# A four-layer spectral network and a dilation on one core: loads placed ahead, accumulations moved by one VectorE operation, other first pairs of a layer

## The chip, the cores and the metric

The kernel runs on one core of a Trainium2 chip. The metric is the device time of the program in microseconds (us), as the median of several executions. The profile is a trace of one further execution. PE is TensorE (its matmuls), PEld its weight loads, DVE VectorE, ACT ScalarE, POOL GpSimd and SP SyncE; SP works on no data here, it issues DMAs.

## What is computed

Eight images of 8 channels and 256x256 pixels, all in 32-bit floats. Each is normalized, goes through a Fourier neural operator with four groups of 10 channels, is added to its input, and is normalized and dilated (the maximum over 3x3 pixels):

```python
h = _gconv1x1(h, fc0_w, fc0_b)
for i in range(4):
    h1 = _spectral_conv(h, sp_w1[i], sp_w2[i])   # rfft2, 12x12 low modes mixed by channel, irfft2
    h2 = _gconv1x1(h, w_w[i], w_b[i])
    h = h1 + h2
    if i < 3:
        h = _gswish(h, betas[i])
h = _gswish(_gconv1x1(h, fc1_w, fc1_b), betas[3])
return _gconv1x1(h, fc2_w, fc2_b)
...
x = x + _L0_conv_ref(_gn(x), ...)
x = x + _L1_conv_ref(_gn(x))
```

## The kernel before

Two streams of work are woven into each other. While the layers of image b run, the head of image b-1 (the two 1x1 convolutions fc1 and fc2) runs beside them, and after it the dilation of image b-2 or b-1, called the tail. Image 0 has no head beside it, and the head of image 7 runs alone at the end.

**The head** is a generator of 128 steps. Step n does `first(n)`: four matmuls of 512 columns (L686) into four PSUM banks, a single one and a group of three, which ACT turns into `act` (L687, L688). Each odd step also does `second(n-3)`: eight matmuls (L708) that take two earlier `act` tiles, and an addition of the result to `y` on DVE (L711 for the first of 16, else L713). Below, F36 is `first(36)`, S34 is `second(34)` and y34 its addition.

**A layer** l of an image has four stages. `spectrum_h` turns the rows of the previous layer with four DVE transposes (L353), multiplies them on PE (`p_b`, L362) and scales the result into B with six small DVE operations (L369). `mix` makes twelve DVE operations in turn, a multiplication with spectral weights (L390) and a sum (L393), then F (L405, L406), the small product `p_f` on PE (L415) and from it `fz`, with one DVE multiplication by a mask `own` (L428). `rows_of` makes `p_g` on PE in three groups (G0, G4, G8; L447 in even layers, L452 in odd ones) and copies them to `zt` (L204). `layer` then makes eleven bursts Z0 to Z10 (`p_z`: L523 in layer 0, where the weights are `wcn`, L526 in the others, then L529), which ACT evicts to `h` (L534); in layers 0 to 2 a pair of bursts is turned by DVE (`turn`, L477), transformed by PE (`transform`, L494: D0 to D5) and gathered (`gather`, L508). For layer 0 of the next image, `start` (its spectrum and its mix) runs beside the end of layer 3.

**The order** on PE, DVE and ACT is the order in which the program is written; the generators' `yield`s say how many head steps go in at that place, `"tail"` takes one step of the tail. The order of SP's queue is left to the framework's scheduler. PSUM has two single banks and two groups of three; a new tile takes the one that was freed first in the program's order, so which wait a matmul gets depends on where the reader of an earlier tile stands. A burst, a head step, `p_d` and `p_g` take one bank of each sort; `p_f`, `p_b`, `p_u` and the result of `second` a single one.

**Loads:** `hs` are chunks of layer 3's result, stored to memory and read back for the head; `y` is the part of the input to which the head adds; `read_x` loads the image for layer 0 into `h`; `load_sw` loads the spectral weights for the mix (three parts; the third goes in when the first is used up).

Of the kernel before, what the change touches and what calls it, by code (L numbers as in the profile page):

```python
# [19 lines left out]
HW = 256  # L20
NPIX = HW * HW
G = 4
# [21 lines left out]
def fno_dilate_kernel(ctx: ExitStack, tc: tile.TileContext, a: dict, out: bass.AP):  # L44
    nc = tc.nc
    mm = nc.tensor.matmul
    PE, DVE, ACT = mybir.EngineType.PE, mybir.EngineType.DVE, mybir.EngineType.Activation

# [74 lines left out]
    nc.vector.memset(fz, 0.0)  # L123
    own = const.tile([128, NQ], F32, tag="own", name="own")
    nc.vector.memset(own, 0.0)
    for i in range(NQ):
        nc.vector.memset(own[part(i), i : i + 1], 1.0)

# [218 lines left out]
    def spectrum_h(b, l, out_):  # L347

        rows = turned.rearrange("p t f -> p (t f)")[:, : NBLK * WID * 128]
        view = rows.rearrange("p (g i k) -> p i g k", g=G, k=32)  # L350
        for g in range(G):

            nc.vector.transpose(  # L353
                rows[:, 960 * g : 960 * (g + 1)].rearrange("p (i r) -> p i r", r=32), windows(g))
            yield (1,) if g < G - 1 else (1, 1)
        p = ps_a(f"p_b_{b}_{l}")
        for k in range(2):
            for n in range(2 * NBLK):
                term, blk = n // NBLK, n % NBLK
                for q in range(4):  # L360
                    k0 = 12 * term + 3 * q
                    mm(p[part(q), 120 * k : 120 * k + 120], eh_f[:, spectrum_table(k, term), blk, :],  # L362
                       view[:, WID * blk : WID * (blk + 1), :, k0 : k0 + 3],
                       start=n == 0, stop=n == 2 * NBLK - 1)
        bt = sb.tile([128, 2, 3, G, WID], F32, tag="B", bufs=1, name=f"B_{b}_{l}")
        s = io[:, 4 * l : 4 * l + 4]
        for part_ in range(2):
            for k in range(3):
                nc.vector.tensor_tensor(  # L369
                    bt[:, part_, k].rearrange("p g i -> p i g"),  # L370
                    p[:, 120 * part_ : 120 * part_ + 120].rearrange(
                        "p (i g k) -> p i g k", i=WID, g=G)[:, :, :, k],
                    s.unsqueeze(1).to_broadcast([128, WID, G]), ALU.mult,
                )
        out_["bt"] = bt
# [6 lines left out]
    def mix(b, l, out_):  # L382
# [3 lines left out]
        for n in range(12):  # L386
            k, k2 = n // 4, n // 2 % 2
            pr = turned[:, 2, 1024 * k2 : 1024 * k2 + 800].rearrange("p (g m i) -> p g m i", g=G, i=WID)
            if n % 2 == 0:
                nc.vector.tensor_tensor(  # L390
                    pr, sw[k], bt[:, k2, k].unsqueeze(2).to_broadcast([128, G, 2 * WID, WID]), ALU.mult)
            else:
                nc.vector.tensor_reduce(  # L393
                    s[k2][:, k].rearrange("p g s o -> p (g s o)"),
                    pr.rearrange("p g m i -> p (g m) i"), AX.X, ALU.add,
                )
            if n == 3:
                sw.append(load_sw(l, 2))
            if l > 0:
                if n not in (2, 6, 10):  # L400
                    yield (1,)
            elif n % 2 or n > 7:
                yield (1,)
        f = sb.tile([128, 2, 3, G, WID], F32, tag="F", bufs=1, name=f"F_{b}_{l}")
        nc.vector.tensor_tensor(f[:, 0], s[0][:, :, :, 0, :], s[1][:, :, :, 1, :], ALU.subtract)  # L405
        nc.vector.tensor_tensor(f[:, 1], s[0][:, :, :, 1, :], s[1][:, :, :, 0, :], ALU.add)  # L406
        if l == 0:
            yield (1,)

        p = ps_a(f"p_f_{b}_{l}")  # L410
        sums = p[:, : 6 * WID * G].rearrange("p (o g s k) -> p s o g k", o=WID, g=G, s=2)
        for slot in range(2):
            for n, (table, part_of) in enumerate(((0, slot), (1 + slot, 1 - slot))):
                for q in range(4):
                    mm(sums[part(q), slot], fold[part(q), table, :],  # L415
                       f[part(q), part_of].rearrange("p k g o -> p o g k"), start=n == 0, stop=n == 1)
        nc.vector.tensor_copy(fz[0:32, :, :, 24], cz[:, l])
# [8 lines left out]
        if l < 2:  # L426
            nc.vector.tensor_copy(fz[0:32, :, :, 25], cz[:, 4 if l == 0 else 3])
        nc.vector.tensor_tensor(  # L428
            fz[:, :, :, : 6 * NQ].rearrange("p o g (q k) -> p (o g) q k", q=NQ),
            p[:, : 6 * WID * G].rearrange("p (n k) -> p n k", k=6).unsqueeze(2).to_broadcast([128, WID * G, NQ, 6]),  # L430
            own.unsqueeze(1).unsqueeze(3).to_broadcast([128, WID * G, NQ, 6]), ALU.mult)

    def rows_of(b, l, side):
# [3 lines left out]
        for os_ in (range(0, 4), range(4, 8), range(8, 10)):  # L437
# [16 lines left out]
            for u, o in enumerate(os_):  # L454
# [7 lines left out]
                copy(u, dst, src)  # L462
            yield (1, 1) if os_[0] == 0 or os_[0] == 8 and l < 3 else (1,)
            if l < 3:
                yield "tail"
            elif os_[0] != 4:
                next(side, None)


    def layer(b, l, out_, stored, side):  # L470
# [68 lines left out]

        def read_x(c):  # L540
            for g in range(G):
                nc.sync.dma_start(
                    h[32 * g : 32 * g + 6, c].rearrange("p f w -> p (f w)"), a["xp"][b, c, g])

        if l == 0:
            for c in range(NCH):
                read_x(c)
            wcn = sb.tile([128, 32], F32, tag="wcn", bufs=1, name=f"wcn_{b}")
            nc.vector.tensor_scalar(wcn, wc, out_["mr"][:, 1:2], None, ALU.mult)
        if l == 3:  # L550
            for c in range(NCH):
# [6 lines left out]
                if c in (0, 1, 2, 5, 6, 7):  # L558
                    yield "tail"
                next(side, None)  # L560
            return
        for k in range((NCH + 1) // 2):
# [3 lines left out]
            if k > 1:  # L566
                gather(k - 2)
            if k == 0 or alone[0]:
                turn(c)
# [6 lines left out]
                continue  # L576
            yield (1,)
            turn(c)
            transform(k - 1)
            for _ in range(2 if k > 1 and pair else 1):  # L580
                yield "tail"
# [12 lines left out]
    def start(b, out_):  # L594
        if b < n_img:
            out_["sw"] = [load_sw(0, 0), load_sw(0, 1)]
            yield from spectrum_x(b, out_)
            yield from mix(b, 0, out_)

    def layers(b, stored, d, then):  # L600

# [3 lines left out]
        for l in range(4):  # L605
            if l > 0:
                yield from spectrum_h(b, l, d)
                if l == 3 and b + 1 < n_img:
                    load_x(b + 1)
                yield from mix(b, l, d)  # L610
            yield from rows_of(b, l, then)
            yield from layer(b, l, d, stored, then)
        yield "stored"
        yield from then

# [48 lines left out]


    def head(b, stored, stats):
        hs, acts, box = {}, {}, {}
# [5 lines left out]
        def load_state(k):  # L673

            if k < NQ * NCH:
                j, c = k // NCH, k % NCH
                hs[k] = sb.tile([128, PIX], F32, tag="hs", bufs=4, name=f"hs_{b}_{k}")
                nc.sync.dma_start(hs[k], stored[c][:, PIX * j : PIX * (j + 1)])

        def first(n):  # L680

            k, blk = n // 32 * NCH + n % 32 // NBLK, n % 32 % NBLK
            act = sb.tile([128, G, 512], F32, tag="act", bufs=4, name=f"act_{b}_{n}")
# [7 lines left out]
        def second(n):  # L691

            t, rb = n // 16, n % 16
            if rb == 0:
                if last:
                    y = ya[:, 1 + 2 * t : 3 + 2 * t, 1 : HW + 1]
                else:
                    y = sb.tile([128, 512], F32, tag="yp", name=f"y_{b}_{t}")
                    y = y.rearrange("p (s w) -> p s w", s=2)
                box["y"] = y  # L700
                nc.sync.dma_start(
                    y, a["x"][b].rearrange("c (p t s w) -> (c p) t s w", p=16, t=8, s=2)[:, t])
            y, acc = box["y"], ps_a(f"p_fc2_{b}_{n}")
            sums = acc.rearrange("p (s w) -> p s w", s=2)
            for i in range(2):
                act = acts.pop(n + i)
                for g in range(G):
                    mm(acc[part(g), :], w2[:, g, 15 - rb - i : 47 - rb - i], act[:, g, :],  # L708
                       start=i == 0, stop=i == 1)
            if rb == 0:  # L710
                nc.vector.scalar_tensor_tensor(y, sums, b2, y, ALU.add, ALU.add)  # L711
# [11 lines left out]

        load_state(0)
        load_state(1)
        yield
        for n in range(STEPS):
# [5 lines left out]
            yield  # L733
        second(STEPS - 2)


# [38 lines left out]

    heads, tails, count = [], [], [0]

    def step():
# [4 lines left out]
        if next(gen, b) is b:  # L783
            heads.pop(0)
            tails.append((dilate if b + 1 < n_img else dilate_last)(b, stats_of.pop(b)))
            return step()
        count[0] += 1
        return True
# [6 lines left out]
    with tc.manual_schedule(engines={PE, DVE, ACT}):  # L795
# [3 lines left out]
        for b in range(n_img):  # L799
            stored = [dram.tile([128, NQ * PIX], F32, tag=f"hs{c}", name=f"stored_{b}_{c}") for c in range(NCH)]  # L800
            ahead = {}
            for n in layers(b, stored, d, start(b + 1, ahead)):
                if n == "stored":
                    if b + 1 < n_img:
                        stats_of[b] = sb.tile([128, 8, 6], F32, tag="bn_y", name=f"bn_y{b}")
                    else:
                        stats_of[b] = spare[:, 16384:16480].rearrange("p (n s) -> p n s", s=6)
                    heads.append((b, head(b, stored, stats_of[b])))
                    next(heads[-1][1])
                    alone[0] = False  # L810
                elif n == "tail":
                    tail()
                elif heads:
                    for _ in n:
                        step()
            d = ahead
        while step():
            tail()
        for t in tails:
# [165 lines left out]
```

## Time and profile before

| | |
|---|---|
| Time, median of 3 runs | 3972.9 us (3970.92 to 3978.73) |
| The profiled execution's own time | 3984.03 us |
| Its span | 3982.2 us |
| Granted TensorE clock, mean | 0.960 |
| DMA traffic | read 213.39 MB, written 123.74 MB |
| One head step, first half: 8 records of L686 | 644 ns mean of one, overlapping |
| ACT on one step: L687 and L688 | 601 and 1456 ns |
| One y addition (L713) | 684 ns |
| One multiplication or sum of the mix (L390, L393) | 982 and 984 ns |

The profiled execution was 11 us longer than the median, 0.3%. Each matmul appears as two records[...]. The records of matmuls overlap, so the time of a stage on PE is read from the start of one group to the start of the next. The page names for each engine what ended its idle time. A granted clock below 1.0 means that TensorE ran at half speed for a part of the stretch.

### The profile page before, as it was taken

How to read it: one execution, taken by the hardware profiler on the slowest of the kernel's cores; microseconds unless marked ns; L12 is line 12 of the kernel's file. 1: busy time of each engine (PE TensorE's matmuls, PEld its weight loads, DVE VectorE, ACT ScalarE, POOL GpSimd, SP SyncE). 2: the span in 40 equal slices, each digit the busy share in tenths (PEclk: the TensorE clock that was granted, in tenths of full speed). 3: DMA queues.
4: the chain of work that ended last, by engine and by line, in shares of the span. 5: the costliest groups of instructions: out<-in, count | busy, mean ns of one | idle time of the engine just before them, and what ended most of it. 6: DMA issues, size and time to landing. Idle time of an engine off the chain costs nothing.

```text
span 3982.2 us, 116980 instructions
## 1 busy us (share of the span) xinstructions
PE 3689.1 (93%) x53114; PEld 1427.5 (36%) x53114; DVE 2443.7 (61%) x3675; ACT 2829.6 (71%) x2923; POOL 116.9 (3%) x202
## 2 busy tenths in 40 slices
PE   5669999999999999999999999999999989999997
PEld 2334333333333333333333333333333333333222
DVE  6665665466675666756666566665666556764643
ACT  3336777767777677776777767777777767778886
POOL 1000000000000000000000000000000000000000
PEclk8879999999999999999999999999999989999998
DMA  3014111432125221261213611135112542115321
GB/s 86 15 47 173 51 41 35 164 95 63 59 85 176 62 61 57 80 212 33 63 54 94 198 36 60 56 123 167 56 43 58 163 121 59 56 44 188 110 70 47
DMA packets 114121, 344.94 MB, mean 87 GB/s; under 512 B 16040, under 2 KB 18536, under 8 KB 98200
## 3 DMA queue, kind: packets, MB, share of 16 engines
q1 hardware_dynamic: 95432, 276.32, 22.3%
q0 software_dynamic: 18192, 61.13, 4.7%
q8 instruction: 418, 6.85, 0.7%
q14 instruction: 79, 0.65, 0.1%
HBM read 213.39 MB, written 123.74 MB: 85 GB/s over the span
## 4 chain that ended last, share of the span: by engine, by line
PE 79%; DVE 11%; issue 4%; ACT 4%; DMA 3%; SPq 0%; POOL 0%; DVEq 0%; POOLq 0%; ACTq 0%
PE p_fc L686 22%; PE p_fc L708 21%; PE p_z L529 9%; PE p_d L494 7%; PE p_z L526 6%; PE p_z L523 3%; PE p_u L508 3%; PE p_b L362 2%; DVE turned L477 2%; PE p_g L452 2%; PE p_g L447 2%; PE p_f L415 2%; DVE turned L353 1%; DVE turned L390 1%; DMA t<-in_spw 1%
## 5 line engine op out<-in xcount | busy, mean ns | idle before, releaser
L688 ACT ACTIVATE act<-p_fc 128x1536 f32<-128x1536 f32 x1024 | 1491.2, 1456 | 1.4 <-PE p_fc L686 1.4
L686 PE MATMUL p_fc<-hs,c_w 32*128 32x512 f32 x8192 | 1183.1, 644 | 49.1 <-DVE y L713 22.0
L708 PE MATMUL p_fc<-act,c_w 128*32 128x512 f32 x8192 | 1003.2, 606 | 5.1 <-ACT act L687 4.7
L687 ACT ACTIVATE act<-p_fc 128x512 f32<-128x512 f32 x1024 | 615.1, 601 | 494.2 <-PE p_fc L686 479.4
L477 DVE STREAM_TRANSPOSE turned<-h 128x1024 f32<-128x1024 f32 x528 | 630.3, 1225 | 322.6 <-ACT h L534 322.4
L534 ACT ACTIVATE h<-p_z 128x512 f32<-128x512 f32 (+1 forms) x528 | 511.8, 1021 | 293.1 <-PE p_z L529 293.1
L713 DVE TENSOR_TENSOR y<-p_fc,y 128x512 f32<-128x512 f32 x392 | 268.2, 684 | 569.8 <-PE p_fc L708 569.6
L686 PEld LDWEIGHTS p_fc<-hs,c_w 32*128 32x128 f32 x8192 | 379.5, 187 | 628.4 <-ACT act L687 226.9
L708 PEld LDWEIGHTS p_fc<-act,c_w 128*32 128x32 f32 x8192 | 216.7, 110 | 733.8 <-issue 366.2
L529 PE MATMUL p_z<-c_binv,zt 32*128 32x256 f32 x5632 | 422.1, 415 | 0.0
L529 PEld LDWEIGHTS p_z<-c_binv,zt 32*128 32x128 f32 x5632 | 264.3, 191 | 318.1 <-issue 305.0
L526 PE MATMUL p_z<-h,c_wt 32*32 32x512 f32 x8448 | 353.5, 599 | 6.2 <-ACT act L687 4.1
L494 PE MATMUL p_d<-turned,c_fw 32*32 32x480 f32 (+1 forms) x9216 | 312.2, 541 | 20.9 <-DVE turned L477 20.6
L498 ACT ACTIVATE turned<-p_d 128x1440 f32<-128x1440 f32 x144 | 183.1, 1271 | 101.7 <-PE p_d L494 98.5
L536 ACT ACTIVATE h<-p_z,c_bias 128x512 f32<-128x512 f32 (+1 forms) x176 | 186.6, 1111 | 71.0 <-PE p_z L529 70.8
L204 DVE COPY zt<-p_g 128x264 f32<-128x264 f32 x300 | 161.9, 617 | 95.2 <-PE p_g L447 42.4
L494 PEld LDWEIGHTS p_d<-turned,c_fw 32*32 32x32 f32 x9216 | 129.3, 103 | 201.7 <-issue 66.8
L390 DVE TENSOR_TENSOR turned<-t,B 128x800 f32<-128x800 f32 x192 | 188.5, 982 | 20.5 <-DMA t<-in_spw 20.4
L393 DVE TENSOR_REDUCE S<-turned 128x80 f32<-128x800 f32 x192 | 189.0, 984 | 5.7
L353 DVE STREAM_TRANSPOSE turned<-zt 128x960 f32<-128x960 f32 x96 | 177.4, 1874 | 2.5
L415 PE MATMUL p_f<-F,c_fold 32*32 32x120 f32 x1024 | 62.1, 391 | 102.7 <-DVE F L405 86.9
L526 PEld LDWEIGHTS p_z<-h,c_wt 32*32 32x32 f32 x8448 | 94.1, 103 | 163.5 <-ACT act L687 59.8
(180 smaller groups left out, 1997.2 us busy)
## 6 DMA issues: line engine op xcount, KB each, us to landing
stored<-h SPq DMA_DIRECT2D x88, 1024.0 KB
hs<-stored SPq DMA_DIRECT2D x352, 256.0 KB
t<-in_spw SPq DMA_DIRECT2D x96, 400.0 KB
yin<-y_rows POOLq DMA_DIRECT2D x56, 512.0 KB, 5.0
h<-in_xp SPq DMA_DIRECT2D x352, 48.0 KB
turned<-in_xw SPq DMA_DIRECT2D x16, 1024.0 KB
y<-in_x SPq DMA_DIRECT2D x56, 256.0 KB
y_rows<-y POOLq DMA_DIRECT2D x56, 256.0 KB, 2.3
```

Of the source, the lines that this page charges most:

```text
L353: nc.vector.transpose(rows[:, 960 * g : 960 * (g + 1)].rearrange("p (i r) -> p i r", r=32), windows(g))
L390: nc.vector.tensor_tensor(pr, sw[k], bt[:, k2, k].unsqueeze(2).to_broadcast([128, G, 2 * WID, WID]), ALU.mult)
L477: nc.vector.transpose(dst[:, 2 * i : 2 * i + 2], h[:, c, 2 * i : 2 * i + 2].rearrange("p f (s x) -> p f s x", s=2))
L494: mm(banks[q][part(v % 4), : 240 * n], fw8[part(q), v, :], t[part(q), :, :, v, : NBLK * WID], start=v < 4, stop=v >= 4)
L526: mm(o, wt[part(q), l, g, :], h[part(q), c, f, :], start=True, stop=False)
L529: mm(banks[q][:, HW * s : HW * (s + 1)], zt[part(q), 2 * c + s].rearrange("p f o -> p (f o)"), binv[part(q), :], start=False, stop=s == 1)
L534: nc.scalar.activation(dst, src, AF.Silu)
L686: mm(banks[g], w1[part(g), blk, :], hs[k][part(g), :], start=True, stop=True)
L687: nc.scalar.activation(act[:, 0, :], one, AF.Silu)
L688: nc.scalar.activation(act[:, 1:4, :], tri, AF.Silu)
L708: mm(acc[part(g), :], w2[:, g, 15 - rb - i : 47 - rb - i], act[:, g, :], start=i == 0, stop=i == 1)
L713: nc.vector.tensor_tensor(y, sums, y, ALU.add)
```

## The change

The description of it reads: loads placed ahead of their use, SyncE's order left to the scheduler; accumulations one VectorE operation later in loose stages; new first pairs of a layer. In detail:

- The addition of `second` is not written out at once but put on the list `sums_due`. `sum_up()` writes it out: at the start of the next `first`, and, where the yield is a tuple, right after the step. A yield of `"late"` (in `spectrum_h` and `mix`) makes a step without that, so that whatever DVE operation is written next stands ahead of the addition.
- `fz` is filled by four copies, one for each quarter of the partitions, two on DVE and two on ACT, in place of one DVE multiplication by `own`; `p_f` is written and read without strides.
- The first pair of bursts of layers 0 to 2: a head step moves from ahead of Z0 to between Z1 and Z2, and D0 moves ahead of the step that it followed.
- The head's first loads (`hs` 0 and 1, `y` 0) are made while layer 3 of its image still runs (`"ready"`), each later `y` eight steps earlier; `read_x` of the next image goes chunk by chunk into layer 3 and the rest; `load_x` moves from before to within the mix of layer 3.

```diff
@@ spectrum_h
-            yield (1,) if g < G - 1 else (1, 1)
+            yield "late"
+        yield "late"
@@ mix
-            if l > 0:
-                if n not in (2, 6, 10):
-                    yield (1,)
-            elif n % 2 or n > 7:
-                yield (1,)
+            if n not in (2, 6, 10) if l > 0 else n % 2 or n > 7:
+                yield "late"
+            if n == 2 and l == 3 and b + 1 < n_img:
+                load_x(b + 1)
...
-        sums = p[:, : 6 * WID * G].rearrange("p (o g s k) -> p s o g k", o=WID, g=G, s=2)
-                    mm(sums[part(q), slot], fold[part(q), table, :],
-                       f[part(q), part_of].rearrange("p k g o -> p o g k"), start=n == 0, stop=n == 1)
+                    mm(p[part(q), 120 * slot : 120 * slot + 120], fold[part(q), table, :],
+                       f[part(q), part_of].rearrange("p k g o -> p (k g o)"), start=n == 0, stop=n == 1)
...
-        nc.vector.tensor_tensor(
-            fz[:, :, :, : 6 * NQ].rearrange("p o g (q k) -> p (o g) q k", q=NQ),
-            p[:, : 6 * WID * G].rearrange("p (n k) -> p n k", k=6).unsqueeze(2).to_broadcast([128, WID * G, NQ, 6]),
-            own.unsqueeze(1).unsqueeze(3).to_broadcast([128, WID * G, NQ, 6]), ALU.mult)
+        for q in range(NQ):
+            dst = fz[part(q), :, :, 6 * q : 6 * q + 6].rearrange("p o g k -> p k g o")
+            src = p[part(q), :240].rearrange("p (k g o) -> p k g o", g=G, o=WID)
+            if q % 2:
+                nc.scalar.activation(dst, src, AF.Identity)
+            else:
+                nc.vector.tensor_copy(dst, src)
@@ rows_of
-            yield (1, 1) if os_[0] == 0 or os_[0] == 8 and l < 3 else (1,)
+            yield (1, 1) if os_[0] == 0 else (1,)
@@ layer
-        if l == 0:
-            for c in range(NCH):
-                read_x(c)
+        if l == 0:
+            for c in range(NCH if b == 0 else 0):
+                read_x(b, c)
...
+                if c in (8, 10):
+                    yield "ready"
+                if c > 3:
+                    read_x(b + 1, c - 4)
...
-            if k == 0 or alone[0]:
+            if alone[0]:
...
-            yield (1,)
-            turn(c)
-            transform(k - 1)
-            for _ in range(2 if k > 1 and pair else 1):
+            if k == 1:
+                transform(0)
+            if k > 0:
+                yield (1,)
+            turn(c)
+            if k > 1:
+                transform(k - 1)
+            for _ in range(min(k, 2) if pair else 1):
                 yield "tail"
@@ head
+    sums_due = []
+    def sum_up():
+        while sums_due:
+            sums_due.pop(0)()
...
         def first(n):
+            sum_up()
...
         def second(n):
-            if rb == 0:
-                ...
-                nc.sync.dma_start(
-                    y, a["x"][b].rearrange("c (p t s w) -> (c p) t s w", p=16, t=8, s=2)[:, t])
+            if rb == 8:
+                load_y(t + 1)
...
+            sums_due.append(lambda: add(t, rb, y, sums))
@@ the main loop
+                if n == "ready":
+                    ...
+                    next(new)
...
                 elif heads:
-                    for _ in n:
+                    for _ in range(1 if n == "late" else len(n)):
                         step()
+                        if n != "late":
+                            sum_up()
```

More of the change, by code (lines that the diff above doesn't have):

```diff
@@ L46, in fno_dilate_kernel @@
     mm = nc.tensor.matmul
-    PE, DVE, ACT = mybir.EngineType.PE, mybir.EngineType.DVE, mybir.EngineType.Activation
+    PE, DVE = mybir.EngineType.PE, mybir.EngineType.DVE
+    ACT = mybir.EngineType.Activation
     const = ctx.enter_context(tc.tile_pool(name="const", bufs=1))
@@ L123, in fno_dilate_kernel @@
     nc.vector.memset(fz, 0.0)
[L124 to L127, printed above, removed]
     def softplus(t, n, name):
@@ L407, in mix @@
         if l == 0:
-            yield (1,)
+            yield "late"
         p = ps_a(f"p_f_{b}_{l}")
-        sums = p[:, : 6 * WID * G].rearrange("p (o g s k) -> p s o g k", o=WID, g=G, s=2)
         for slot in range(2):
@@ L467, in rows_of, with read_x @@
                 next(side, None)
+    def read_x(b, c):
+        if b < n_img:
+            for g in range(G):
+                nc.sync.dma_start(h[32 * g : 32 * g + 6, c].rearrange("p f w -> p (f w)"), a["xp"][b, c, g])
     def layer(b, l, out_, stored, side):
@@ L538, in burst @@
                 nc.sync.dma_start(stored[c], h[:, c].rearrange("p f w -> p (f w)"))
-        def read_x(c):
-            for g in range(G):
-                nc.sync.dma_start(
-                    h[32 * g : 32 * g + 6, c].rearrange("p f w -> p (f w)"), a["xp"][b, c, g])
         if l == 0:
-            for c in range(NCH):
-                read_x(c)
+            for c in range(NCH if b == 0 else 0):
+                read_x(b, c)
             wcn = sb.tile([128, 32], F32, tag="wcn", bufs=1, name=f"wcn_{b}")
@@ L576, in layer @@
                 continue
-            yield (1,)
+            if k == 1:
+                transform(0)
+            if k > 0:
+                yield (1,)
             turn(c)
-            transform(k - 1)
-            for _ in range(2 if k > 1 and pair else 1):
+            if k > 1:
+                transform(k - 1)
+            for _ in range(min(k, 2) if pair else 1):
                 yield "tail"
@@ L598, in start, with rest @@
             yield from mix(b, 0, out_)
+    def rest(b, then):
+        c = NCH - 4
+        for n in then:
+            yield n
+            if c < NCH:
+                read_x(b + 1, c)
+                c += 1
+        for i in range(c, NCH):
+            read_x(b + 1, i)
     def layers(b, stored, d, then):
@@ L607, in layers @@
                 yield from spectrum_h(b, l, d)
-                if l == 3 and b + 1 < n_img:
-                    load_x(b + 1)
                 yield from mix(b, l, d)
@@ L613, in layers @@
         yield "stored"
-        yield from then
+        yield from rest(b, then)
     spare = h.rearrange("p c f w -> p (c f w)")
@@ L678, in load_state, with load_y @@
                 nc.sync.dma_start(hs[k], stored[c][:, PIX * j : PIX * (j + 1)])
+        def load_y(t):
+            if t < 8:
+                if last:
+                    y = ya[:, 1 + 2 * t : 3 + 2 * t, 1 : HW + 1]
+                else:
+                    y = sb.tile([128, 512], F32, tag="yp", name=f"y_{b}_{t}")
+                    y = y.rearrange("p (s w) -> p s w", s=2)
+                box[t] = y
+                nc.sync.dma_start(
+                    y, a["x"][b].rearrange("c (p t s w) -> (c p) t s w", p=16, t=8, s=2)[:, t])
         def first(n):
+            sum_up()
             k, blk = n // 32 * NCH + n % 32 // NBLK, n % 32 % NBLK
@@ L693, in second @@
             t, rb = n // 16, n % 16
-            if rb == 0:
[L695 to L701, printed above, removed]
-                    y, a["x"][b].rearrange("c (p t s w) -> (c p) t s w", p=16, t=8, s=2)[:, t])
-            y, acc = box["y"], ps_a(f"p_fc2_{b}_{n}")
+            if rb == 8:
+                load_y(t + 1)
+            y, acc = box[t], ps_a(f"p_fc2_{b}_{n}")
             sums = acc.rearrange("p (s w) -> p s w", s=2)
@@ L709, in second, with add @@
                        start=i == 0, stop=i == 1)
+            sums_due.append(lambda: add(t, rb, y, sums))
+        def add(t, rb, y, sums):
             if rb == 0:
@@ L724, in head @@
         load_state(0)
+        yield
         load_state(1)
+        load_y(0)
         yield
@@ L773, in dilate @@
             yield
-    heads, tails, count = [], [], [0]
+    heads, tails = [], []
     def step():
@@ L786, in step @@
             return step()
-        count[0] += 1
         return True
@@ L800, in fno_dilate_kernel @@
             stored = [dram.tile([128, NQ * PIX], F32, tag=f"hs{c}", name=f"stored_{b}_{c}") for c in range(NCH)]
-            ahead = {}
+            ahead, new = {}, None
             for n in layers(b, stored, d, start(b + 1, ahead)):
[L803 to L809, printed above, removed]
+                if n == "ready":
+                    if new is None:
+                        if b + 1 < n_img:
+                            stats_of[b] = sb.tile([128, 8, 6], F32, tag="bn_y", name=f"bn_y{b}")
+                        else:
+                            stats_of[b] = spare[:, 16384:16480].rearrange("p (n s) -> p n s", s=6)
+                        new = head(b, stored, stats_of[b])
+                    next(new)
+                elif n == "stored":
+                    heads.append((b, new))
                     alone[0] = False
@@ L813, in fno_dilate_kernel @@
                 elif heads:
-                    for _ in n:
+                    for _ in range(1 if n == "late" else len(n)):
                         step()
+                        if n != "late":
+                            sum_up()
             d = ahead
         while step():
+            sum_up()
             tail()
```

## The prediction

> **What bounds the kernel.** I read the page's shares first, then busy time by stretch, then what PE waits for, then one mix line by line.
>
> ```profile
> PE 3689.1 (93%) x53114; PEld 1427.5 (36%) x53114; DVE 2443.7 (61%) x3675; ACT 2829.6 (71%) x2923; POOL 116.9 (3%) x202
> ```
> ```profile
> 0.00:330.00 330.00, 207.91 (x4446) 109.75 (x4446) 222.89 (x366) 116.32 (x124) 11.25 (x26) 0.84 0.19 58
> ...
> 1710.00:2170.00 460.00, 437.08 (x6164) 166.20 (x6160) 289.20 (x422) 330.77 (x341) 13.38 (x22) 0.96 0.28 87
> ...
> 3800.00:3983.00 183.00, 154.09 (x1228) 44.84 (x1228) 71.16 (x127) 141.81 (x151) 4.77 (x8) 0.92 0.19 56
> ```
>
> PE sets the end. Columns of a stretch: length, busy PE, PEld, DVE, ACT, POOL, then PE clock, DMA share, GB/s. In a steady image of 460 us PE idles about 20 us and has clock 0.96 to 0.98; DMA is used at 0.28. Matmul work is hardly changed, so the change can give only PE's idle time and the half-speed time. Summing (1 - clock) over 330 to 3830 us gives 97 us, in steps of 1.71.
>
> ```profile
> PE p_f L415 <- DVE F L405: 86.9, 26, 13.1
> PE p_fc L686 <- DVE y L713: 22.0, 7, 5.7
> PE p_d L494 <- DVE turned L477: 20.6, 17, 1.4
> ...
> PE p_z L523 <- DVE wcn L549: 14.3, 7, 3.4
> ```
>
> Total us, times, longest. Counted in the steady part: p_f waits 2.13 us 21 times (layers 1 to 3, seven images), D0 waits 1.43 us 14 times. The line L686 <- y is the passage from image to image, where DVE itself waits for the third load of the weights.
>
> ```profile
> 445.71 1.96 DVE L353 STREAM_TRANSPOSE turned<-zt 128x960 f32<-128x960 f32 x1
> ...
> 448.37 0.69 DVE L713 TENSOR_TENSOR y<-p_fc,y 128x512 f32<-128x512 f32 x1 [0.71 <-PE p_fc L708]
> 448.98 3.71 DVE L353 STREAM_TRANSPOSE turned<-zt 128x960 f32<-128x960 f32 x2
> ...
> 459.74 1.76 PE L686 MATMUL p_fc<-hs,c_w 32*128 32x512 f32 x12
> 459.88 0.76 DVE L369 TENSOR_TENSOR B<-p_b,io 128x40 f32<-128x40 f32 x6 [2.80 <-PE p_b L362]
> ...
> 475.60 1.14 PE L686 MATMUL p_fc<-hs,c_w 32*128 32x512 f32 x8
> 475.74 0.75 DVE L711 SCALAR_TENSOR_TENSOR y<-p_fc,c_b,y 128x512 f32<-128x512 f32 x1 [0.66 <-PE p_fc L708]
> 476.40 0.98 DVE L390 TENSOR_TENSOR turned<-t,B 128x800 f32<-128x800 f32 x1
> ...
> 478.87 1.94 PE L415 MATMUL p_f<-F,c_fold 32*32 32x120 f32 x32 [2.13 <-DVE F L405]
> ```
> ```profile
> 459.70:473.70 14.00, 14.00 (x114) 4.24 (x112) 11.48 (x19) 12.25 (x14) 0.55 (x1) 1.00 0.33 98
> 478.00:485.00 7.00, 6.13 (x56) 2.10 (x56) 2.23 (x6) 2.63 (x3) 0.00 (x0) 0.76 0.35 99
> ```
>
> DVE stands still for 0.7 us before an addition (the transpose stopped at 447.67, the addition began at 448.37): it waits for a sum that PE has not finished. Eight such pauses make F late, and p_f waits. After the stall the clock is 0.76 over 7 us: 0.24 x 7 = 1.7 us more. This half-speed window follows 19 of the 21 stalls; none follows D0's.
>
> **What the Trainium skill says.** "TensorE: Matmul & The Clock Gate", section "What's actually happening", names two clocks, half and full, judged by free-running windows of 3413 ns. The trace agrees: a window at half speed loses 1.71. The page lets the clock fall after a window of idleness; here 2.13 us sufficed, and the trace decides. "PSUM — Partial Sum Buffer", section "Engine vs sequencer instructions", calls VectorE a strict FIFO and has matmuls start in program order. So an addition that is moved back gives its bank back later, and everything on PE behind the matmul that takes that bank waits too; the passages (L686 <- y) show it. "Perfetto Trace Analysis", "Tensor Engine Instruction", says that matmul ends are estimated, so I use starts.
>
> **The change, part by part**, against the profiled execution (3984.0 us; the median is 11.1 less).
>
> A. Late additions, 21 times. Worked on the mix above. t0 and t1 now run together, 445.71 + 3.71 = 449.42, y20 ends 450.04. F25, which needs y20's bank and was ready at 449.2, stalls 0.88. t2 and t3 end 453.75, y22 454.35: F27 stalls 0.5 (0.3 before). p_b thus starts at 457.2, not 456.13 (+1.07). F28's bank is now p_b's, free only after the sixth B: a stall of 0.94 (0.76 of B, the rest latency). PE is 2 us late at 461.75, but the mix no longer pauses: S28 469.7, S32 477.65, the last sum 478.0, y32 478.65, F 478.86, p_f at 479.03 against 478.87. So p_f's stall falls to 0.3, and 1.8 us of it reappears earlier: net -0.16. S34 now also waits for ACT's copies of fz behind act(36), 0.35. Without the half-speed window, 1.71 x 19/21 = 1.55; I keep one in ten of them: 1.39. Per mix 1.39 - 0.16 - 0.35 = 0.88; x 21 = **18.6**. That the window goes is the unmeasured part. For it: stalls of 1.43 never caused one, and the new ones are at most 0.94, with p_b's dense stream between; against it: they follow each other. Both ends: no window lost (gain 22), or a second one (see the rivals).
>
> B. Layer 0's mix runs in the loose end of layer 3, and at the passages SP has the third load of weights in the same place: 0.
>
> C. First pair of layer 0, seven times. Before, F11 and S8 came ahead of Z0, and DVE made wcn behind S8's addition: Z0 waited 1.0 to 3.4 us for it, 14.3 in all, and in image 1 started 9.15 us after G8. Now F11 and S8 stand after Z1, nothing is ahead of wcn, and Z0 starts 5.25 after G8, when its banks come free (read off the same rows in the new order); then F11 and S8 take 2.9 to 3.1. Gain 9.15 - 5.25 - 3.1 = 0.8, less 0.45 for Z3, whose bank waits for ACT's eviction of D0, now later in its queue: 0.35 x 7 = 2.5. Z0 to Z2 in a row, with K = 6, are followed by two to four half-speed windows (38.7 us in all); with head steps between them I take one fewer each, 1.7 x 7 = 12, the least measured term. Sum **14.5** (2 to 25).
>
> D. First pair of layers 1 and 2, 14 times. A head step goes in ahead of Z2, so the second half of the turn has y40 ahead of it and is ready 12.0 us after G8, while PE gets to D0 at 11.5: stall 0.5 in place of 1.43. Less 0.45 at Z3: 0.48 x 14 = **6.7**. The wait of a head step for the copies to zt (3.7 in all) moves to Z0, same size.
>
> E. fz: DVE's one operation of 1.16 becomes two copies and two on ACT. Straight from L687 and L688 (512 elements 0.60, 1536 elements 1.45), 240 elements are 0.37 each, an estimate. Only the four mixes of image 0, with no head, feel it: **+1**. The unstrided p_f is 32 matmuls of the same size: 0.
>
> F. Loads. A y tile has two buffers, so its load is released at the same event as before, with eight steps to spare in either; read_x and hs have long slack at 0.28 DMA use. This queue is in order, and only at the first passage do I find loads moved behind stores (hs 0 behind stored 8, the weights behind stored 9): hs some 3 to 6 us later, partly under a wait of 3.04 that is there already: **-2** (-8 to 0).
>
> Sum: 18.6 + 14.5 + 6.7 + 1 - 2 = 39, so the profile 3984 becomes 3945 and the median 3972.9 becomes **3934**. Next late are then the passages (22 us) and what is left of wcn.
>
> **Rivals.**
>
> R1, no change: the half-speed windows stay, because the window counts idle time wherever it lies and the mix keeps 2.3 us of it. 21 x (-0.51) + 2.5 + 6.7 + 1 - 2 = -2.5 the wrong way: 3975. For it: the sum of stalls is nearly the same; against it: they are spread over 30 us, about nine windows.
>
> R2, slower: F28 behind B. PE stands idle after p_b until the sixth B is read, and trips a half-speed window in every mix, while p_f's wait stays long enough to keep its own. 21 x (0.51 + 1.71) = 46.6 lost, 8 gained: +38, 4011. It decides once that stall is over about 1.3 us, between the 1.43 that D0 shows harmless (ahead of dense work) and the 2.13 of p_f, since p_b's matmuls are small. For it: F28 must wait by its bank; against: B's row is 0.76 in all.
>
> R3, much faster: the waits for additions hide behind PE's queue, and p_f's stall goes whole: 21 x (2.13 + 1.55) + 14 x 1.43 + 14.5 = 112, so 3861. Against it: F25's wait, worked out above, has nothing beside it on an in-order PE.
>
> **How the numbers follow.** Forecast 0.52, R1 0.15, R2 0.22, R3 0.11. The forecast's own range is 3905 to 3962: the terms at their low ends (A 11 with one window in three kept, C 2, D 3, F -5, so 11) or high (A 22, C 25, D 20 with its stall gone, E 1, so 68). Less than 0.2% (8 us) can't be told from no change. Faster: 0.95 of the forecast, R3 and some of R1, 0.62; same 0.15; slower, nearly all R2, 0.23. The range leaves out the far half of R3 and the upper half of R2: 3888 to 4005.
>
> **What would show it.** Right: p_f <- F under 0.5 each, new waits of p_fc L686 on y L713 and on B of under 1 us, 21 each, clock 1.0 after p_f; D0's 1.43 down to 0.5; fewer half-speed windows after Z2 of layer 0. Wrong: clock 0.5 within 5 us of p_b (R2), stretches of 0.76 still after p_f (R1), or no wait at F25 (R3). The forecast falls if the passages grow by more than 10 us, which I hold for unchanged.

## The result: no change that can be measured

The changed kernel takes 3974.6 us (median of 12 runs, 3963.44 to 3982.1) against 3972.7 before: ratio 1.0002, 95% interval 0.999 to 1.0014. The forecast was 3934, its range 3888 to 4005. Its profiled execution took 3980.3 us, with a span of 3978.2.

The page's shares, one steady image, and what PE waits for, in the changed kernel (columns as before; lines of code have moved, L686 to L721, L708 to L736, L713 to L745, L523 to L527):

```profile
PE 3648.8 (92%) x53114; PEld 1397.8 (35%) x53114; DVE 2428.8 (61%) x3702; ACT 2866.7 (72%) x2987; POOL 117.0 (3%) x202
```
```profile
1710.00:2170.00 460.00, 430.81 (x6235) 162.29 (x6231) 287.81 (x429) 340.35 (x354) 13.39 (x22) 0.98 0.29 91
```
```profile
PE p_f L411 <- DVE F L402: 46.9, 24, 12.9
PE p_fc L736 <- ACT fz L428: 40.6, 28, 1.7
PE p_fc L721 <- DVE y L745: 35.9, 27, 6.9
PE p_fc L721 <- ACT act L722: 25.0, 51, 0.7
PE p_fc L721 <- DVE B L367: 20.4, 21, 1.0
...
PE p_z L527 <- DVE wcn L548: 12.6, 8, 3.0
PE p_fc L721 <- DMA hs<-stored: 12.1, 2, 7.9
```

The change did what it says. p_f waits 40 us less, D0's waits for its turn fall from 20.6 us to 0.4, wcn waits a little less, and the clock of the image is 0.98 in place of 0.96. Yet PE idles more: 179 us from 330 to 3830 us, before 144. Four waits that the list of before does not have, or has smaller, take all that p_f and D0 gave, and more: for fz (40.6), for B (20.4), for ACT (25.0 against 10.6) and for hs (12.1). Summed over one-microsecond windows, (1 - clock) fell from 97 us to 60 in that stretch, so the gain of the clock and the loss of idle time seem to cancel. But PE's busy time fell by only 40 us in all, and some 29 of them (an estimate: 0.92 us in each of 32 mixes) come from p_f's shorter matmuls, as the experiments show. So the 97 us were not all real.

The starts of p_f also say where the time goes. At the first passage, before and then in the changed kernel:

```profile
353.48 1.94 PE L415 MATMUL p_f<-F,c_fold 32*32 32x120 f32 x32 [3.04 <-DVE F L405]
```
```profile
373.09 1.02 PE L411 MATMUL p_f<-F,c_fold 32*32 32x120 f32 x32
```

The changed kernel is 19.6 us late there. It is 6.9 late already at the last mix of image 0 (p_f at 304.00, before at 297.10), and 12.7 come at the passage. From there to the end it wins 23.6 us, by these two profiles.

One mix in the changed kernel's timeline:

```profile
463.56 1.14 PE L721 MATMUL p_fc<-hs,c_w 32*128 32x512 f32 x8 [0.64 <-DVE y L745]
...
475.20 1.14 PE L721 MATMUL p_fc<-hs,c_w 32*128 32x512 f32 x8 [0.97 <-DVE B L367]
...
477.04 2.00 PE L721 MATMUL p_fc<-hs,c_w 32*128 32x512 f32 x8 [0.70 <-ACT act L722]
...
494.87 1.02 PE L411 MATMUL p_f<-F,c_fold 32*32 32x120 f32 x32 [0.40 <-DVE F L402]
...
495.95 0.56 DVE L430 COPY fz<-p_f 32x240 f32<-32x240 f32 x1 [0.84 <-PE p_f L411]
496.54 0.56 ACT L428 ACTIVATE fz<-p_f 32x240 f32<-32x240 f32 x1
...
497.14 0.56 DVE L430 COPY fz<-p_f 32x240 f32<-32x240 f32 x1 [0.63 <-ACT fz L428]
497.73 0.56 ACT L428 ACTIVATE fz<-p_f 32x240 f32<-32x240 f32 x1 [0.62 <-DVE fz L430]
...
498.34 1.93 PE L736 MATMUL p_fc<-act,c_w 128*32 128x512 f32 x16 [1.38 <-ACT fz L428]
```

Read the brackets. F25's wait for y20, F28's for B and p_f's for F are those of the forecast (0.88, 0.94 and 0.3 there). Two are not. F29 waits 0.70 for ACT, which had run empty behind F28's wait. And the four copies of fz don't run side by side: each waits for the one before on the other engine, they start 0.60 us apart, and S34 stands 1.38 us for the last.

### The profile page after: what moved, and what is told of

It reads as the page before. It is cut to its first block, busy times and chain, and to the rows that moved or that the text cites. A ratio compares the mean times of both kernels' runs of the same rounds, so it can differ in the third digit from the quotient of the medians.

```text
span 3978.2 us, 117004 instructions
## 1 busy us (share of the span) xinstructions
PE 3648.8 (92%) x53114; PEld 1397.8 (35%) x53114; DVE 2428.8 (61%) x3702; ACT 2866.7 (72%) x2987; POOL 117.0 (3%) x202
## 4 chain that ended last, share of the span: by engine, by line
PE 77%; DVE 12%; issue 4%; ACT 4%; DMA 2%; POOL 0%; SPq 0%; DVEq 0%; POOLq 0%; ACTq 0%
PE p_fc L721 20%; PE p_fc L736 19%; PE p_z L533 9%; PE p_z L530 8%; PE p_d L498 7%; DVE turned L350 3%; PE p_u L512 3%; PE p_z L527 3%; PE p_b L360 2%; PE p_g L446 2%; PE p_g L451 2%; DVE y L745 1%; DVE turned L388 1%; DVE S L391 1%; ACT act L722 1%
## 5 line engine op out<-in xcount | busy, mean ns | idle before, releaser
L721 PE MATMUL p_fc<-hs,c_w 32*128 32x512 f32 x8192 | 1162.1, 638 | 104.9 <-DVE y L745 35.9
L736 PE MATMUL p_fc<-act,c_w 128*32 128x512 f32 x8192 | 1003.1, 606 | 40.6 <-ACT fz L428 40.6
L721 PEld LDWEIGHTS p_fc<-hs,c_w 32*128 32x128 f32 x8192 | 363.4, 185 | 684.3 <-ACT act L722 223.6
L745 DVE TENSOR_TENSOR y<-p_fc,y 128x512 f32<-128x512 f32 x392 | 267.3, 682 | 473.5 <-PE p_fc L736 473.3
L736 PEld LDWEIGHTS p_fc<-act,c_w 128*32 128x32 f32 x8192 | 216.8, 110 | 764.4 <-issue 395.1
L530 PE MATMUL p_z<-h,c_wt 32*32 32x512 f32 x8448 | 363.6, 600 | 8.4 <-ACT act L722 4.1
L428 ACT ACTIVATE fz<-p_f 32x240 f32<-32x240 f32 x64 | 36.1, 564 | 149.9 <-DVE fz L430 146.8
```

Source lines behind the costliest of these rows:

```text
L530: mm(o, wt[part(q), l, g, :], h[part(q), c, f, :], start=True, stop=False)
L721: mm(banks[g], w1[part(g), blk, :], hs[k][part(g), :], start=True, stop=True)
L745: nc.vector.tensor_tensor(y, sums, y, ALU.add)
```

## The experiments

Each ran beside the kernel before, whose medians were 3972.7 to 3973.9 us. Two groups: the changed kernel with one part undone or mended, and the kernel before with one part of the change alone.

| | edit | us | ratio to before | 95% interval |
|---|---|---|---|---|
| b_late | before, late additions | 3985.2 | 1.0033 | 1.0019 to 1.0047 |
| b_pairs | before, first pairs | 3939.7 | 0.9922 | 0.9902 to 0.9942 |
| b_fz | before, copies of fz and unstrided p_f | 3990.4 | 1.0049 | 1.0031 to 1.0067 |
| b_loads | before, loads | 3987.3 | 1.0038 | 1.0025 to 1.0051 |
| a_own | changed, fz and p_f as before | 3970.1 | 0.9987 | 0.9977 to 0.9996 |
| a_own2 | changed, one multiplication, p_f unstrided | 3946.5 | 0.9937 | 0.9914 to 0.9961 |
| a_dve4 | changed, all four copies on DVE | 3960.3 | 0.9965 | 0.9949 to 0.998 |
| a_sum24 | changed, y24 at once | 3941.3 | 0.9907 | 0.9889 to 0.9925 |
| a_reads | changed, image 1's reads later | 3966.8 | 0.9987 | 0.9977 to 0.9997 |
| b_late24 | before, late additions but y24 | 3943.6 | 0.9929 | 0.9911 to 0.9947 |
| a_best2 | a_own2, a_sum24 and a_reads together | 3900.3 | 0.9821 | 0.9796 to 0.9845 |
| b_best | as a_best2, loads as before | 3886.5 | 0.9785 | 0.9767 to 0.9803 |

**fz: a_own, a_dve4, a_own2 and b_fz.** a_own takes the diff's hunks on fz and p_f back. a_dve4 has

```diff
-            if q % 2:
-                nc.scalar.activation(dst, src, AF.Identity)
-            else:
-                nc.vector.tensor_copy(dst, src)
+            nc.vector.tensor_copy(dst, src)
```

> The changed kernel with fz filled by one DVE multiplication again (and p_f in the old layout). Theory: the four copies of fz run one after another (0.56 us each, DVE and ACT in turn, 2.34 us) where the multiplication took 1.16, and S34, which takes p_f's bank, waits 1.38 to 1.65 us for the last, 29 times, 42 us. With the multiplication S34 waits about 0.25: a gain of some 35, and 3 in image 0: 3936, ratio to the kernel before 0.991. Rival: DVE bounds the mix, so the time comes back as a later y34 or p_f: gain under 10, 3966 or more.

> The changed kernel with all four copies of fz on DVE. Theory (what counts is that the copies follow one another): four copies of about 0.5 us end as late as now, S34 still waits 1.2 to 1.5 us for fz, time within 8 us of the changed kernel's 3974. Rival (what counts is ACT, whose queue holds the copies behind act(36) and act(37) behind the copies): S34's wait falls below 0.7, time 3950 or less.

S34's wait fell from 1.38 to 0.20 in a_own, as the theory has it, but the time fell by 4.5 us and not by 38, which is hardly clear of the noise (the intervals of a_own and of the changed kernel overlap). The rows of p_f, by tile, say why: the first line is of the kernel before, the second of the changed one (min, median, max in ns).

```profile
L415 PE MATMUL p_f<-F,c_fold x1024: 370/392/405, 51.5 to 3598.5; 32*32 32x120 f32 x171
```
```profile
L411 PE MATMUL p_f<-F,c_fold x1024: 257/261/405, 51.5 to 3594.5; 32*32 32x120 f32 x171
```

The same 32 matmuls take PE 1.94 us strided and 1.02 unstrided. The change had won 0.9 us a mix with the layout, and a_own gave it back. In a_dve4 the copies still take 2.34 us on DVE alone, so two engines that take turns are no faster than one (what makes the program order the copies so isn't shown); but S34 then takes act(36)'s bank and waits 0.67 for ACT, and ACT's act(37) no longer stands behind them. It gained 14 us, between the two expectations: each was half right. a_own2 keeps the good half of each, with F stored in the order in which it is read:

```diff
-        f = sb.tile([128, 2, 3, G, WID], F32, tag="F", ...)
+        f = sb.tile([128, 2, 3, WID, G], F32, tag="F", ...)
...
+            p[:, : 6 * WID * G].rearrange("p (k n) -> p n k", k=6).unsqueeze(2).to_broadcast([128, WID * G, NQ, 6]),
+            own.unsqueeze(1).unsqueeze(3).to_broadcast([128, WID * G, NQ, 6]), ALU.mult)
```

> The changed kernel with fz filled by one DVE multiplication, but p_f unstrided as in the change (F is stored in the order in which it is read). Theory: the unstrided p_f takes PE 1.02 us, the strided one 1.94, so the change gained 0.9 in each of 32 mixes there and lost it again to the four copies; with both, S34's wait is about 0.25 in place of 1.38 and p_f stays short: 30 to 36 less than the changed kernel, 3938 to 3945, ratio 0.991 to 0.993. Rival: reading p_f in another order makes the multiplication, or F's operations, longer by what is won: 3960 or more.

> The kernel before with the four copies of fz and the unstrided p_f alone. Theory: S34 waits 1.4 to 1.65 us for the last copy 28 times (40), the unstrided p_f gives back 0.9 each (26), and a half-speed window that began under p_f now lies over more matmuls: 10 to 18 more, 3983 to 3991. Rival: the two even out, 3970 to 3979.

a_own2 gained 28 us on the changed kernel, a little less than the 30 to 36 expected; p_f's median stays at 261 ns and the multiplication at 1.16 us. b_fz lies in its range, 17 more than before, but not by the sum expected: its waits at S34 are 28.9 us and not 40, which the unstrided p_f (26) nearly pays. In the profiles it is 6 us longer than before, and 7 late by the last mix of image 0, where p_g's waits for fz grow from 5.3 us to 10.0; the rest of the 17 is not placed.

**The late additions: b_late, a_sum24 and b_late24.** b_late is the diff's `sums_due`, `sum_up` and `"late"` alone. In the other two one yield differs:

```diff
             yield "late"
-        yield "late"
+        yield (1,)
         p = ps_a(f"p_b_{b}_{l}")
```

> The kernel before with the late additions alone (list of sums, yields of late in spectrum_h and mix). Theory, from the rows of the changed kernel: p_f's waits fall from 48 to 9 us, but F25 waits for y20 (21 x 0.64), F28 for B (21 x 0.97) and F29 for ACT (21 x 0.70): 49 us new, so idle time is up by 9; the half-speed windows after p_f (34 us) become some 12: together 13 us less, 3960, ratio 0.9967. Rival 1: this part gains nothing (3970 or more) and the clock is no better. Rival 2: it is what gained, and other parts lost: 3945 or less.

> The changed kernel, but the last step before p_b writes its addition (y24) at once, so it stands on DVE ahead of B, where DVE idles 6.7 us, and F28 takes y24's bank and not p_b's. Theory: F28's wait for B (0.97 x 21 = 20) and the wait of F29 for ACT behind it (0.70 x 21 = 15) both go, and with them the half-speed windows at that place (12): 30 to 45 less, 3930 to 3944, p_f's wait for F still about 0.4. Rival: the mix is bound by DVE, so p_f's wait for F grows by what the others lose: gain under 8.

> The kernel with the late additions alone, but y24's addition at once. Theory: as in the changed kernel, F28's wait for B (20) and F29's for ACT (15) go: 33 less than with all additions late, 3952, ratio 0.9948, so that the late additions gain 20 once y24 is left out. Rival: p_f's wait for F comes back without the other edits: 3970 or more.

b_late came out 12 us slower where 13 less were expected. Its waits are those of the expectation:

```profile
PE p_f L413 <- DVE F L403: 47.0, 24, 13.0
PE p_fc L691 <- DVE y L721: 36.4, 27, 5.6
PE p_fc L691 <- ACT act L692: 24.9, 51, 0.7
...
PE p_fc L691 <- DVE B L370: 20.4, 21, 1.0
```

and its half-speed windows fell from 97 to 67 us. The fault lay in what a window was thought to cost. Two mixes of the kernel before, from the start of p_f to the start of G0, without a window and with one (columns as in the windows before: length first, clock third from the end):

```profile
2521.98:2528.12 6.14, 5.93 (x65) 2.08 (x65) 2.00 (x4) 1.94 (x2) 0.00 (x0) 1.00 0.51 151
478.87:486.16 7.29, 7.29 (x65) 2.38 (x65) 2.08 (x5) 1.94 (x2) 0.00 (x0) 0.77 0.28 87
```

The difference is 1.15 us where (1 - clock) says 1.7. Over the 19 mixes with a window the stretch is 7.08 in the mean, over the two without it 6.14: a window cost 0.94. (In b_late, where no window falls there, all 21 such stretches take 6.13 or 6.14.) p_f itself runs from start to the next head step in 1.87 us at either clock, and S34 has a wait of 0.20 that absorbs some. So 19 windows cost 18 us, not 32. Against those 18 and the 40 that p_f gave stand 53 of new waits (F25 13, F28 20, F29 15, and 0.20 for fz at each S34) and three windows behind F29: by the profiles nothing is won (spans 3982.8 and 3982.2). From the first transpose to G0 a mix takes 40.16 us before and 40.33 in b_late, means of 21, so the mixes cost 4 us more. The profile of before was itself 11 us above its median; the 12 us between the medians are not all placed.

a_sum24 moved y24's addition to where DVE stands idle before B. Its timeline:

```profile
468.90 0.69 DVE L745 TENSOR_TENSOR y<-p_fc,y 128x512 f32<-128x512 f32 x1 [3.12 <-PE p_fc L736]
472.27 2.18 PE L721 MATMUL p_fc<-hs,c_w 32*128 32x512 f32 x16
472.41 0.76 DVE L367 TENSOR_TENSOR B<-p_b,io 128x40 f32<-128x40 f32 x6 [2.82 <-PE p_b L360]
```

F28 starts ahead of B with no wait, F29 (in the same row) follows without a pause, and the kernel is 33 us faster, as expected; against the expectation p_f's 0.40 goes too. b_late24 confirms it without the other parts: late additions without this one gain 29 us (20 were expected), with it they lose 12. Its mixes take 38.51 us.

**First pairs: b_pairs**, the diff's hunks in `rows_of` and `layer` (for layers 0 to 2) alone.

> The kernel before with the new first pairs of layers 0 to 2 alone. Theory: D0's wait (14 x 1.43 = 20) nearly goes, less 3 at Z3; wcn's waits fall by some 5 and the half-speed windows behind the bursts of layer 0 from 39 to 17 us: 40 to 44 less, 3930 to 3934, ratio 0.990. Rival: what D0 no longer waits for comes back at Z0, Z3 or the next pair: 3960 or more.

33 us faster, where 40 to 44 were expected. D0's wait and the zt wait ahead of it are gone from its list, p_f's stays:

```profile
PE p_f L415 <- DVE F L405: 86.2, 26, 13.3
...
PE p_z L523 <- DVE wcn L549: 12.5, 7, 3.0
```

The half-speed time behind wcn's waits in layer 0 fell from 39 us to 17. These windows count for more than p_f's. In b_pairs layer 0 takes, from the start of Z0 to that of D1, 22.32 us without one, 25.13 with 3.41 us of (1 - clock) and 26.77 with 5.12: over these bursts some 0.85 of it is real.

**Loads: b_loads and a_reads.** In b_loads PE, DVE and ACT have before's order and only SP's queue differs. a_reads lets image 1's reads start after layer 3:

```diff
-                if c > 3:
+                if c > 3 and b > 0:
                     read_x(b + 1, c - 4)
...
-        c = NCH - 4
+        c = NCH - 4 if b > 0 else 0
```

> The kernel before with the change's loads alone: the order of PE, DVE and ACT is that of before, only SP's differs. Theory: it costs what the first passage shows in the changed kernel, two waits for hs of 12.1 us with 3.9 at half speed, less the 3.0 and 1.7 that stood there before: +11, 3984, ratio 1.0028; the other passages as before. Rival 1: hidden by the wait for the weights, 3976 or less. Rival 2: the parts measured so far leave some 17 to the loads, so other passages got worse as well: 3988 or more.

> The changed kernel, but image 1's reads of x (read_x) go in after the head's first loads; those of the other images stay. Theory: the two waits of the head of image 0 for hs at 350 to 367 us (7.88 and 4.21 us, with 3.9 us at half speed after them) come from SP's queue, where hs 0 stands behind stored 8 and behind reads of x: they shrink to 4 or less together, 3964 to 3967. Rival: hs is late by the transfer itself, or the third load of the weights holds DVE there anyway: no change, 3971 or more.

b_loads lost 14 us (11 were expected), a_reads won 8 back, in its range. SP's queue in the changed kernel at the first passage (the name after the line is the DMA's target and source):

```profile
349.80 0.35 SPq L542 DMA_DIRECT2D stored<-h  x1
350.52 0.35 SPq L700 DMA_DIRECT2D hs<-stored  x1
350.96 3.37 SPq L472 DMA_DIRECT2D h<-in_xp  x4
354.42 0.35 SPq L542 DMA_DIRECT2D stored<-h  x1
...
358.96 0.35 SPq L542 DMA_DIRECT2D stored<-h  x1
359.36 0.42 SPq L700 DMA_DIRECT2D hs<-stored  x1
```

Before, the first load of hs followed the first store:

```profile
313.33 0.33 SPq L538 DMA_DIRECT2D stored<-h  x1
318.25 0.33 SPq L678 DMA_DIRECT2D hs<-stored  x1
```

Here it is issued at 350.52, behind the ninth store, with reads of x around it, and the head's first matmul waits until 357.61 (7.88 us) and its matmuls again until 367.02 (4.21). In a_reads it is issued at 326.59, right after the first store, and both waits are gone; p_f waits 5.52 us at the same place for an addition instead, so about half of the loss stays.

**Together: a_best2 and b_best.**

> The changed kernel with three edits: y24's addition at once, image 1's reads after the head's first loads, and the one multiplication with the unstrided p_f. Theory: the three gains lie at different places and add up: 33 + 8 + 32 = 73 less than the changed kernel, 3900, ratio 0.981 to 0.983. Rival: with one wait gone the next takes its place (the mix becomes bound by DVE): 3925 or more.

> The kernel before with the new first pairs, the late additions but y24, and the one multiplication with the unstrided p_f, loads as before: PE, DVE and ACT have the same order as in the changed kernel with its three edits (3900), only SP's differs. Theory: the change's loads gain nothing, so 3893 to 3902. Rival: the loads placed ahead are worth something once the rest is quicker: 3908 or more.

a_best2 is at 3900, as expected; its parts alone (33, 28 and 8 us) make some 3905. b_best is at 3886, below the 3893 to 3902 expected. They are 1.8 and 2.1% faster than the kernel before, but each rests on four runs. Their spans in the profile are equal, 3891.0 and 3891.1, and their intervals overlap a little, so whether the loads cost 14 us even then isn't settled.

## Why the prediction was wrong

*The sum.* Forecast and measured alone (ratio less one, times 3972.7): late additions -26 without fz's 0.35, measured +13; first pairs -21, measured -31; fz and p_f +6, measured +19; loads +2, measured +15. The four alone make +16, the whole change +1. The intervals of the four, taken together, are some 13 to either side, so that difference is hardly clear of the noise. The sign of three parts was right; the largest term had the wrong one. By place, in the profiles: the 21 mixes were to give 19 us and cost 16 (40.16 us each before, 40.93 after); the way to the first p_f of image 1 was to cost 1 and cost 20; the rest was to give 21 and gave 40.

*A, the step that failed.* "Without the half-speed window, 1.71 x 19/21 = 1.55; I keep one in ten of them: 1.39." The windows after p_f did go, all 19 of them; in 7 mixes, where the forecast allowed for 2, there is now one after F29. But 1.71 was the clock's loss over the whole window, as if PE had been limited by its clock all through it; measured over the mix it was 0.94. The windows after F29 lie over matmuls that do run slower: from p_b to p_f the changed kernel takes 24.37 us with one (mean of 7) and 22.71 without (mean of 14), so each costs 1.66. So 29 us of the forecast shrank to some 6 (18 less 7 x 1.66). The idle terms were near one by one (F25 0.64 for 0.88, F27 none for 0.5, F28 0.97 for 0.94, p_f 0.40 for 0.3), but F29's 0.70 behind F28 was missing: 15 us.

*A and E, the copies.* "S34 now also waits for ACT's copies of fz behind act(36), 0.35" is the second failure: 1.38, 21 times, and 1.65 in layer 0. I took the two engines as working side by side and 0.37 us a copy; they take turns, 0.56 each. "32 matmuls of the same size: 0" for p_f was wrong the other way, by 0.9 us a mix, and so hid the copies' cost in a_own. E's gain of 1 us in image 0 was a loss: p_g's waits for fz there are 4.7 us longer.

*B* holds as far as the waits show: those for y, 22.0 us before, are 22.5 once F25's 13.4 are taken off. *C and D* came out better than forecast, 31 and not 21: D0's stall went but for some 0.2 each, and Z3's wait of 0.45 for ACT did not appear (the trace has 1.1 us of waits for h in all).

*F* said -2 with an end at -8. It saw the place, the order and the wait that was there before, but put the lateness of hs at 3 to 6 us; it was 7.9, and 4.2 again for the next chunk.

*The rivals.* R1's time (3975) is the measured one, but not its reason: it kept the windows, and they went. So the hit is luck. R2 came true in part: with F29's 0.70 behind it, F28's 0.97 brought a window in 7 mixes, under the 1.3 that it named (the trace of before has windows behind single waits of 1.01 to 1.27 already, in layer 0); p_f's own wait fell to 0.40. R3 fell with F25's wait. "The forecast falls if the passages grow by more than 10 us" came true at the first one.

The two clocks that the Trainium skill names ("TensorE: Matmul & The Clock Gate", section "What's actually happening") are the trace's: every clock record is 1.0 or 0.5. How much of a half-speed window is lost depends here on the matmuls that lie under it.

## What to carry to other kernels

Price a half-speed window by the stretch it covers, with and without it, and not by its clock: of the same 1.71 us it cost 0.94 at p_f, some 1.45 over layer 0's bursts and 1.66 over the head's matmuls. The strided p_f, and waits, lost nothing. When an accumulation is moved back, ask which bank the next matmuls take; keep at once the one addition that stands where its engine is idle anyway, and move the others. Splitting one operation over two engines pays only if the program lets them run together; look at the starts of the pieces, not at their lengths.

## What the runs showed of the hardware

The same 32 matmuls of 120 columns take 392 ns a record with strided operands and 261 without; whether the stride in the result or in F does it isn't separated by any run. The strided p_f took 1.87 us from its start to the next head step's at full and at half clock; the unstrided one took 0.95 at full clock and 1.75 when 0.88 us of (1 - clock) lay over it (b_fz). A wait of 0.97 followed by one of 0.70 within 2 us was followed by a half-speed window in 7 of 21 mixes of the changed kernel and in 3 of 21 of b_late. Before, the 14 single waits of 1.43 at D0 had none after them, but all six of 1.01 to 1.27 in layer 0 (for wcn, an eviction's bank or mv_y) had one: the length of a single wait doesn't decide it. Over the 80 runs of the kernel before, the time rises by some 0.8 us with each us of (1 - clock).
